# Cross-attention queries made in two steps of 128 columns in place of one step of 256

## The chip, the cores and the metric

One core of a Trainium2 chip runs the whole program. The metric is the time of one execution on the device, in microseconds; the time before is the median of three runs. The profile is of one further execution, with every instruction of the engines recorded: TensorE (PE, with its weight loads as PEld), VectorE (DVE), ScalarE (ACT), GpSimd (POOL) and SyncE (SP), which issues the transfers.

## What is computed

Two layers of a transformer block with self attention, attention to a context, and a gated feed-forward. Everything is float32. `x` is 4 x 512 x 320, the context 4 x 1601 x 192; there are 20 heads of 16.

```python
def _attn(x, ctx, wq, wk, wv, wo, bo, heads):
    q = (x @ wq).reshape(b, n, heads, dh).transpose(0, 2, 1, 3)
    k = (ctx @ wk).reshape(b, j, heads, dh).transpose(0, 2, 1, 3)
    v = (ctx @ wv).reshape(b, j, heads, dh).transpose(0, 2, 1, 3)
    sim = jnp.einsum('bhid,bhjd->bhij', q, k) * scale
    a = jax.nn.softmax(sim, axis=-1)
    out = jnp.einsum('bhij,bhjd->bhid', a, v)
    return out.transpose(0, 2, 1, 3).reshape(b, n, heads * dh) @ wo + bo
...
h1 = _ln(x, n1_g, n1_b)
x = _attn(h1, h1, q1, k1, v1, o1_w, o1_b, heads) + x
h2 = _ln(x, n2_g, n2_b)
x = _attn(h2, context, q2, k2, v2, o2_w, o2_b, heads) + x
h3 = _ln(x, n3_g, n3_b)
a, g = jnp.split(h3 @ ff_w1 + ff_b1, 2, axis=-1)
x = a * gelu(g) @ ff_w2 + ff_b2 + x
```

## The kernel before

**Units.** Attention is cut into units: one batch and one group of four heads. Each layer has 20 self units (4 batches x 5 groups), then 20 cross units, then 4 feed-forward units. A self unit has 512 keys in 4 chunks of 128, a cross unit 1601 keys in 13 chunks, the last of 65.

**Scores twice.** Each unit's scores are made twice. First as `sps` tiles (128 queries x up to 512 keys), of which DVE takes the maximum (`pm`, `nmax`); then as `st` tiles (128 keys x 512 queries), with a third product that subtracts the maximum (`nrows` by `ones`), of which ACT makes the exponential `pr`. The `sps` tiles of the next unit are made beside the `st` tiles of this one. A number is split into a high and a low part, so each tile is two products on 32 rows (and the third for `st`).

**Rounds.** `main` goes chunk by chunk. In one round it issues the `st` tiles of the chunk for four heads (12 products), mixed with four `sps` tiles of the next unit (8 products, `round_of`); then `flush` issues the product `av` of the chunk before with the values; then `steps(None, ...)` issues small steps, so that these stand between an `av` and the next round. ACT copies `av` to `vo`, and POOL adds it to `o`. For the rows of the order below, an `av` row opens a round's end: what is listed between it and the next `st` are the steps.

**Steps.** All preparation for coming units is cut into steps that wait in chains: `norm` and `scale` (layer norms), `context`, `proj` and `early` (keys, `kps`, and queries, `qps`, of cross units; both together, `qkps`, for self units), `values` (`vps`), `divide` and `project` (`ops`). A step of a chain has a cost in us, a due round, and a test whether it may run. `pace` works out from costs and due rounds how much credit a round gets; `pick` takes the head of the chain that is due first; `steps` runs it if the credit covers a share of its cost (0.5, 0.75, then 1.5 times the cost, `share`). So a smaller step needs less credit to run, and the order of all steps follows from the costs. A step's products go to one of eight PSUM banks; `bank` takes the one that a small time model (`written`, `busy`) expects to be free first. ACT copies it out.

**Queries of a cross unit.** `queries` multiplies the normed tokens `first.hT` by `wq2` for the unit's 64 columns. The 512 tokens are two halves `i` of 256, which go to two pairs of 32-row slots, so a step is 3 (rows of the contraction) x 2 x 2 = 12 products of 256 columns. In the trace each is two records, 24. ACT copies the bank with a factor to the low part of a staging tile `halves`, POOL makes of it the high and the low part (`split`, lines 827 and 828), and two transfers on SP's queue move them to `q` (`move_queries`, line 876). The moves wait for the buffer's last reader (`unread`) and `u.when` is set when all are issued; a unit's `sps` tiles start four rounds later (`at_hand`). Where the tiles are due and the queries are not made, `at_once` runs the chain and the moves on the spot.

Of the kernel before, what the change touches and what calls it, by code (L numbers as in the profile page):

```python
# [19 lines left out]
H, DH = 20, 16  # L20
# [3 lines left out]
P = 128  # L24
# [3 lines left out]
SLOT = 32  # L28
GT = GD // SLOT
# [49 lines left out]
def kernel(ctx: ExitStack, tc: tile.TileContext, x, context, ws, out):  # L79
# [18 lines left out]
    nc = tc.nc  # L98
# [314 lines left out]
    def bank(name):  # L413
        i = min(range(NB), key=lambda i: bank_free[i])
        assert bank_free[i] < HELD, name
        t = psum.tile([P, 512], F32, tag=f"bank{i}", name=name)
        bank_of[id(t)] = [i, t, bank_free[i], 0.0]
        bank_free[i] = HELD
        return t

    def written(us, *tiles):
        expect["pe"] = max([expect["pe"]] + [bank_of[id(t)][2] + 0.05 for t in tiles]) + us
        for t in tiles:
            bank_of[id(t)][3] = expect["pe"] + 0.17

    def busy(engine, us, *tiles):
        expect[engine] = max([expect[engine]] + [bank_of[id(t)][3] + 0.05 for t in tiles]) + us
        for t in tiles:
            bank_free[bank_of[id(t)][0]] = expect[engine] + 0.09
# [12 lines left out]
    def add(chain, cost, f, due, ready=yes, soon=yes):  # L442
        chains[chain].append((cost if isinstance(cost, tuple) else (cost,), due, ready, soon, f))
# [348 lines left out]
    def lead(u):  # L792

        if u.i == 0:
            return 0
        return units[u.i - (AHEAD - 1 if u.early else 2 if u.m == 0 else 1)].start
# [28 lines left out]
    def split(low, high):  # L825

        nc.gpsimd.tensor_copy(high.bitcast(F32R), low)
        nc.gpsimd.tensor_tensor(low, low, high, ALU.subtract)

    def add_proj(u):  # L830
        chain = "early" if u.early else "proj"

        due = lead(u) - (9 if u.cross else 24)
        keys_due = due - 10 if u.cross else due
        first = units[u.i - u.g]
# [26 lines left out]
        def staged(w):  # L862
            users.append(u)
            return two.tile([P, 2 * N], F32, tag="halves", name="halves")[:, : 2 * w].rearrange("p (d n) -> p d n", d=2)
# [22 lines left out]
        def staging_free():  # L887
            return len(users) < 2 or not users[-2].moves["q"] and (start["on"] or clock["round"] >= users[-2].moving["q"] + 4)

        def keys_free():  # L890
            return not pending["k"]

        def move_queries(halves, cols, may, gap):
            n = halves.shape[0]
            src = halves.rearrange("p (o d) n -> p o (d n)", o=1).to_broadcast([n, 2, 2 * halves.shape[2]])
            move("q", lambda: [(u.q.rearrange("p d n -> p (d n)")[:, cols], src)], may, gap)
# [38 lines left out]
            first.made["q"] += 1  # L935
            first.made["k"] += 1

        def queries():

            w = N // 2  # L940
            ps = bank("qps")
            written(1.41, ps)
            busy("act", 0.33, ps)
            for k, _, n in HK:
                for i in range(2):
                    for f in range(GT):
                        nc.tensor.matmul(  # L947
                            ps[(i * GT + f) * SLOT : (i * GT + f + 1) * SLOT, :w],
                            lhsT=wq2[:n, k, u.g * GD + f * SLOT : u.g * GD + (f + 1) * SLOT],
                            rhs=first.hT[:n, k, i * w : (i + 1) * w],  # L950
                            start=(k == 0),
                            stop=(k == 2),
                        )
            halves = staged(w)
            high, low = (halves[:, d] for d in range(2))
            nc.scalar.mul(low, ps[:, :w], DH**-0.5)
            split(low, high)
            for i in range(2):
                rows = slice(i * GD, (i + 1) * GD)
                move_queries(halves[rows], slice(i * N, (i + 1) * N), unread, 0 if i else GAP)  # L960
            u.keyed = True
            first.made["q"] += 1

        def keys_of_context(part):

            at, w = KCUT[part]
            ps = bank("kps")
            written(0.1 + w * 4 * 2 / 2400, ps)
            for k in range(2):
                for i in range(2):  # L970
                    for f in range(GT):
                        nc.tensor.matmul(  # L972
                            ps[(i * GT + f) * SLOT : (i * GT + f + 1) * SLOT, :w],
                            lhsT=wk2[:, k, u.g * GD + f * SLOT : u.g * GD + (f + 1) * SLOT],
                            rhs=first.kvT[:, k, i * HALF + at : i * HALF + at + w],
                            start=(k == 0),
                            stop=(k == 1),
                        )
            high, low = (room["halves"][:, d] for d in range(2))
            taken(low[:, at : at + w], ps[:, :w], ps, 0.12 + w * 0.001)  # L980
            if part + 1 < len(KCUT):
                return
            split(low, high)

            def half(i):
                return [(u.kT[:, i * HALF : (i + 1) * HALF], room["halves"][i * GD : (i + 1) * GD])]

            move("k", lambda: half(0), free, GAP + 1)
            move("k", lambda: half(1), free)
            first.made["kv"] += 1  # L990
# [7 lines left out]
        if not u.cross:  # L998
            for part in range(2):
                add(chain, (0.46,) * 3, lambda part=part: both(part), due - 2 + 2 * part, lambda part=part: part or staging_free())  # L1000
        else:
            for part, (_, w) in enumerate(KCUT):
                add(
                    chain, 0.05 + w * 8 / 2400, lambda part=part: keys_of_context(part),
                    keys_due - 2 * (len(KCUT) - 1 - part), lambda part=part: part or keys_free(),
                )
            if u.g == 0:
                add(chain, 0.0, hold, due - (6 if u.g == 0 and not u.early else 4), yes, lambda: "h" in u.own)
            add(chain, (0.477,) * 3, queries, due - (4 if u.g == 0 and not u.early else 2), staging_free)

    def taken(to, part, ps, us):

# [676 lines left out]

    add_norms(0)  # L1690
    add_proj(units[0])
    warm(5)
    until(lambda: not chains["proj"], "proj")
    at_once(units[0])
    add_proj(units[1])
    add_values(units[0])
    run("proj")
    run("proj")
    for _ in range(2 * NQ + 2):
        run("norm")  # L1700
    at_once(units[1])
    add_proj(units[2])
    first = units[0]
    first.pairs = max_pairs(first)
# [68 lines left out]
```

## Time and profile before

| | |
|---|---|
| median of three runs | 2921.99 us (2918.47 to 2926.42) |
| the profiled execution | 2916.39 us, span 2914.6 us |
| mean granted TensorE clock | 0.995 of full speed |
| cross units, first layer | about 381 to 1177 us of the span, 39 to 48 us each but for the last two |
| cross units, second layer | about 1828 to 2615 us |

Times of the trace are counted from the first instruction. A row of the timeline has start, length, engine, line, operation and tiles; records of the same kind that follow each other are put together with their count. A row of the stretches has its start and end, its length, then each engine's busy time with the number of its instructions. In a row of the groups, after the bar, stand busy time, mean length in ns, and idle time before with what ended it. In the list of waits stand the total in us, how often, and the longest.

### The profile page before, as it was taken

How to read it: one execution, taken by the hardware profiler on the slowest of the kernel's cores; microseconds unless marked ns; L12 is line 12 of the kernel's file. 1: busy time of each engine (PE TensorE's matmuls, PEld its weight loads, DVE VectorE, ACT ScalarE, POOL GpSimd, SP SyncE). 2: the span in 40 equal slices, each digit the busy share in tenths (PEclk: the TensorE clock that was granted, in tenths of full speed). 3: DMA queues.
4: the chain of work that ended last, by engine and by line, in shares of the span. 5: the costliest groups of instructions: out<-in, count | busy, mean ns of one | idle time of the engine just before them, and what ended most of it. 6: DMA issues, size and time to landing. Idle time of an engine off the chain costs nothing.

```text
span 2914.6 us, 83287 instructions
## 1 busy us (share of the span) xinstructions
PE 2860.1 (98%) x35018; PEld 1545.0 (53%) x35018; DVE 1975.7 (68%) x3752; ACT 1950.2 (67%) x4033; POOL 1299.4 (45%) x1409
## 2 busy tenths in 40 slices
PE   8999999999999999999999999999999999999999
PEld 4445555555555555355554555555555555544554
DVE  7777888788788878323257678787778878862221
ACT  3777678888888888500138776788888888893000
POOL 3656345555645545211125653455455464551100
PEclk8999999999999999999999999999999999999999
DMA  4444223232132222200113432222221122122000
GB/s 106 114 121 102 72 71 97 58 89 60 48 96 59 55 54 63 85 17 11 36 45 88 109 99 67 61 64 57 54 66 47 50 73 60 45 65 67 23 21 13
DMA packets 163495, 188.59 MB, mean 65 GB/s; under 512 B 61989, under 2 KB 109105, under 8 KB 163121
## 3 DMA queue, kind: packets, MB, share of 16 engines
q1 hardware_dynamic: 162616, 181.69, 24.4%
q8 instruction: 275, 4.51, 0.6%
q10 hardware_dynamic: 472, 1.58, 0.2%
q14 instruction: 100, 0.81, 0.1%
q0 software_dynamic: 32, 0.00, 0.0%
HBM read 55.76 MB, written 29.36 MB: 29 GB/s over the span
## 4 chain that ended last, share of the span: by engine, by line
PE 88%; DVE 4%; POOL 4%; DMA 2%; issue 1%; ACT 1%; SPq 0%; POOLq 0%; ACTq 0%; DVEq 0%
PE av L1350 22%; PE st L1324 20%; PE fps L1435 10%; PE sps L1076 9%; PE yps L1542 6%; PE vps L1035 5%; PE kps L972 4%; PE ops L1250 3%; PE qkps L908 3%; PE fps L1495 3%; DVE nmax L1087 2%; PE qps L947 2%; PE sps L1101 1%; POOL o L1370 1%; DVE pm L1087 1%
## 5 line engine op out<-in xcount | busy, mean ns | idle before, releaser
L1334 ACT ACTIVATE pr<-st 128x512 f32<-128x512 f32 (+1 forms) x2720 | 1405.0, 603 | 321.4 <-PE st L1324 292.0
L1087 DVE TENSOR_REDUCE pm<-sps 128x1 f32<-128x512 f32 (+1 forms) x1920 | 1148.3, 660 | 244.6 <-PE sps L1076 239.0
L1370 POOL TENSOR_TENSOR o<-o,vo 128x512 f32<-128x512 f32 x576 | 739.9, 1285 | 930.3 <-ACT vo L1369 909.7
L1076 PE MATMUL sps<-kT,q 32*128 32x450 f32 (+1 forms) x4800 | 870.6, 422 | 8.1 <-DMA q<-halves 4.4
L1324 PE MATMUL st<-q,kT 32*128 32x512 f32 (+1 forms) x5120 | 788.9, 419 | 0.8 <-ACT o L1364 0.4
L1350 PE MATMUL av<-pr,vals 128*32 128x512 f32 (+1 forms) x5440 | 734.2, 606 | 27.3 <-ACT pr L1334 5.4
L1324 PEld LDWEIGHTS st<-q,kT 32*128 32x128 f32 (+1 forms) x5120 | 447.0, 180 | 293.0 <-issue 112.7
L1324 PE MATMUL st<-nrows,ones 32*128 32x512 f32 (+1 forms) x2720 | 560.6, 398 | 4.5 <-DMA nrows<-turned 4.4
L1087 DVE TENSOR_REDUCE nmax<-sps 128x1 f32<-128x512 f32 x640 | 397.2, 682 | 118.0 <-PE sps L1076 114.2
L1076 PEld LDWEIGHTS sps<-kT,q 32*128 32x128 f32 x4800 | 434.0, 184 | 67.1 <-ACT pr L1334 11.7
L1369 ACT COPY vo<-av 128x512 f32<-128x512 f32 x576 | 351.7, 611 | 14.7 <-PE av L1350 8.7
L1506 ACT ACTIVATE gl<-fps,b 128x512 f32<-128x512 f32 x80 | 54.8, 687 | 408.8 <-PE fps L1495 299.1
L1435 PE MATMUL fps<-hT,w 128*128 128x512 f32 x640 | 283.1, 597 | 0.0
L1350 PEld LDWEIGHTS av<-pr,vals 128*32 128x32 f32 (+1 forms) x5440 | 111.0, 108 | 300.3 <-DVE pm L1087 185.2
L1324 PEld LDWEIGHTS st<-nrows,ones 32*128 32x128 f32 (+1 forms) x2720 | 262.3, 180 | 14.5 <-DMA nrows<-turned 6.1
L1507 DVE SCALAR_TENSOR_TENSOR hid<-fps,b,gl 128x512 f32<-128x512 f32 x80 | 59.7, 748 | 248.1 <-ACT gl L1506 246.0
L1435 PEld LDWEIGHTS fps<-hT,w 128*128 128x128 f32 x640 | 119.2, 190 | 155.1 <-issue 152.2
L1542 PE MATMUL yps<-w,hid 128*128 128x320 f32 x640 | 175.7, 434 | 0.0
L1542 PEld LDWEIGHTS yps<-w,hid 128*128 128x128 f32 x640 | 120.5, 190 | 56.3 <-ACT gl L1506 5.3
L1250 PEld LDWEIGHTS ops<-wo,aT 112*32 112x32 f32 (+1 forms) x3072 | 98.2, 110 | 59.2 <-issue 28.5
L1250 PE MATMUL ops<-wo,aT 112*32 112x160 f32 (+1 forms) x3072 | 123.8, 299 | 3.7 <-POOL aT L1232 2.7
L1111 DVE TENSOR_REDUCE pm<-sps 128x4 f32<-128x508 f32 x160 | 98.9, 680 | 37.5 <-PE sps L1101 34.8
(89 smaller groups left out, 2453.7 us busy)
## 6 DMA issues: line engine op xcount, KB each, us to landing
kT<-stages SPq DMA_DIRECT2D x80, 400.5 KB
oway<-o SPq DMA_DIRECT2D x80, 256.0 KB
q<-halves SPq DMA_DIRECT2D x80, 256.0 KB
q<-halves SPq DMA_DIRECT2D x27, 512.0 KB
kT<-halves SPq DMA_DIRECT2D x40, 256.0 KB
aT<-oway SPq DMA_DIRECT2D x32, 224.0 KB
rT<-rway SPq DMA_DIRECT2D x32, 224.0 KB
hT<-hturned SPq DMA_DIRECT2D x96, 64.0 KB
```

Of the source, the lines that this page charges most:

```text
L972: nc.tensor.matmul(ps[(i * GT + f) * SLOT : (i * GT + f + 1) * SLOT, :w], lhsT=wk2[:, k, u.g * GD + f * SLOT : u.g * GD + (f + 1) * SLOT], ...
L1035: nc.tensor.matmul(ps[f : f + m, :w], lhsT=u.kvT[:n, k, at + f : at + f + m], rhs=wv[:n, k, h0 * DH : h1 * DH], start=(k == 0), stop=(k == ...
L1076: nc.tensor.matmul(own[0][:, :w], lhsT=u.queries(slice(j * SLOT, (j + 1) * SLOT), e, t), rhs=u.kT[j * SLOT : (j + 1) * SLOT, u.k0 + at : u ...
L1087: nc.vector.tensor_reduce(to, own[0][:, :w], AX.X, ALU.max)
L1250: nc.tensor.matmul(ps[f : f + m, : D // 2], lhsT=aT[:n, k, f * NQ + t * SLOT : f * NQ + t * SLOT + m], rhs=wo[:n, k, cols], start=(k == 0) ...
L1324: nc.tensor.matmul(own[0][:r, :], lhsT=ones[rows, :r] if e == 2 else u.keys(rows, c), rhs=u.rows[rows, :] if e == 2 else u.queries(rows, e ...
L1334: nc.scalar.activation(p[:r], own[0][:r], AF.Exp)
L1350: nc.tensor.matmul(ps[j * SLOT : (j + 1) * SLOT, :], lhsT=columns_of[:r, head : head + SLOT], rhs=pr.pop((c, j))[:r, :], start=True, stop= ...
L1369: nc.scalar.copy(vo, ps)
L1370: nc.gpsimd.tensor_tensor(u.o, u.o, vo, ALU.add)
L1435: nc.tensor.matmul(ps, lhsT=w1[:, k, i * FF + c * P : i * FF + (c + 1) * P], rhs=natural(u.hT[:, k]), start=start, stop=stop,)
L1542: nc.tensor.matmul(ps[:, :D], lhsT=hid[c][:, t * P : (t + 1) * P], rhs=w2[:, c, :], start=(c == 0), stop=(c == NHC - 1),)
```

## The change

The step of 256 columns becomes two steps of 128, `queries(0)` and `queries(1)`. Each takes a bank of its own, makes 12 products of 128 columns (columns 0 to 127 of each half of 256, then 128 to 255), and has its own ACT copy into its columns of the same staging tile. Only the second runs the split and queues the moves, and only it marks the unit as keyed. The staging tile is taken by the first, which alone waits for it to be free. In the chain one entry of 3 x 0.477 = 1.431 us becomes two of 0.715 with the same due round.

```diff
-        def queries():
+        def queries(part):
 
             w = N // 2
+            cols = slice(part * P, (part + 1) * P)
             ps = bank("qps")
-            written(1.41, ps)
-            busy("act", 0.33, ps)
+            written(0.72, ps)
+            busy("act", 0.27, ps)
             for k, _, n in HK:
                 for i in range(2):
                     for f in range(GT):
                         nc.tensor.matmul(
-                            ps[(i * GT + f) * SLOT : (i * GT + f + 1) * SLOT, :w],
+                            ps[(i * GT + f) * SLOT : (i * GT + f + 1) * SLOT, :P],
                             lhsT=wq2[:n, k, u.g * GD + f * SLOT : u.g * GD + (f + 1) * SLOT],
-                            rhs=first.hT[:n, k, i * w : (i + 1) * w],
+                            rhs=first.hT[:n, k, i * w + part * P : i * w + (part + 1) * P],
                             start=(k == 0),
                             stop=(k == 2),
                         )
-            halves = staged(w)
+            if part == 0:
+                u.stage = staged(w)
+            halves = u.stage
             high, low = (halves[:, d] for d in range(2))
-            nc.scalar.mul(low, ps[:, :w], DH**-0.5)
+            nc.scalar.mul(low[:, cols], ps[:, :P], DH**-0.5)
+            if part == 0:
+                return
             split(low, high)
...
-            add(chain, (0.477,) * 3, queries, due - (4 if u.g == 0 and not u.early else 2), staging_free)
+            for part in range(2):
+                add(
+                    chain, 0.715, lambda part=part: queries(part),
+                    due - (4 if u.g == 0 and not u.early else 2), yes if part else staging_free,
+                )
```

Because the costs set the order, other steps move too. TensorE in the first layer's eleventh cross unit, its third round, before: the step stands between `av` and the round's first `st` and `sps` tiles (a row names the output and what it is made from, the output's shape, and how many follow each other).

```order
L1350 MATMUL av<-pr,vals 32x512 x4
L947 MATMUL qps<-hT,wq_113 32x256 x12
L1324 MATMUL st<-q_103,kT_101 128x512 x2
L1076 MATMUL sps<-kT_135,q_104 128x450
L1076 MATMUL sps<-kT_135,q_104 128x512
```

Of the change, TensorE in the same unit one round earlier, where no step stood before:

```order
L1359 MATMUL av<-pr,vals 32x512 x4
L948 MATMUL qps<-hT,wq_113 32x128 x12
L1333 MATMUL st<-q_103,kT_101 128x512 x2
L1085 MATMUL sps<-kT_135,q_104 128x450
L1085 MATMUL sps<-kT_135,q_104 128x512
```

The first half stands one round earlier than the wide step stood; the second half stands in that step's old round.

ACT shows several rounds in few rows, since each round has four exponentials and the copy of `av` (to `o` for a unit's first chunk, to `vo` after that), and each TensorE step has its copy behind that of `av`. The same unit's first rounds on ACT, before:

```order
L1364 COPY o<-av 128x512
L1017 COPY vals<-vps 128x8x16
L1334 ACTIVATE pr<-st 128x512 x4
L1369 COPY vo<-av 128x512
L1334 ACTIVATE pr<-st 128x512 x4
L1369 COPY vo<-av 128x512
L956 ACTIVATE halves<-qps 128x256
L1334 ACTIVATE pr<-st 128x512 x4
L1369 COPY vo<-av 128x512
L1334 ACTIVATE pr<-st 128x512 x4
```

and of the change:

```order
L1373 COPY o<-av 128x512
L1026 COPY vals<-vps 128x8x16
L1343 ACTIVATE pr<-st 128x512 x4
L1378 COPY vo<-av 128x512
L959 ACTIVATE halves<-qps 128x128
L1343 ACTIVATE pr<-st 128x512 x4
L1378 COPY vo<-av 128x512
L959 ACTIVATE halves<-qps 128x128
L1343 ACTIVATE pr<-st 128x512 x4
L1378 COPY vo<-av 128x512
```

Of the four rounds, two held no step before; now one does. The second place is ACT one unit earlier, the tenth cross unit, from the end of the ninth. Before:

```order
L1334 ACTIVATE pr<-st 128x512 x4
L1364 COPY o<-av 128x512
L956 ACTIVATE halves<-qps 128x256
L1334 ACTIVATE pr<-st 128x512 x4
L1369 COPY vo<-av 128x512
L1334 ACTIVATE pr<-st 128x512 x4
L1369 COPY vo<-av 128x512
L1334 ACTIVATE pr<-st 128x512 x4
L1369 COPY vo<-av 128x512
L1017 COPY stages<-kps 128x201
```

and of the change:

```order
L959 ACTIVATE halves<-qps 128x128
L1343 ACTIVATE pr<-st 128x512 x4
L1373 COPY o<-av 128x512
L1343 ACTIVATE pr<-st 128x512 x4
L1378 COPY vo<-av 128x512
L959 ACTIVATE halves<-qps 128x128
L1343 ACTIVATE pr<-st 128x512 x4
L1378 COPY vo<-av 128x512
L1343 ACTIVATE pr<-st 128x512 x4
L1378 COPY vo<-av 128x512
L1026 COPY stages<-kps 128x201
```

The first half went ahead to the last round of the unit before, and the second half one round later than the wide step; the round of the copy to `o` and the one before `stages` hold no step.

## The prediction

> **What bounds the kernel now.** I read the page first: the busy shares, then the chain that ended last.
>
> ```profile
> span 2914.6 us, 83287 instructions
> PE 2860.1 (98%) x35018; PEld 1545.0 (53%) x35018; DVE 1975.7 (68%) x3752; ACT 1950.2 (67%) x4033; POOL 1299.4 (45%) x1409
> PE 88%; DVE 4%; POOL 4%; DMA 2%; issue 1%; ACT 1%; SPq 0%; POOLq 0%; ACTq 0%; DVEq 0%
> ```
>
> TensorE is busy for 98% of the span and holds 88% of the chain, so a gain must come out of TensorE's own time. ACT and DVE show about two thirds over the whole span, but that is a mean over stages. So the second view is the busy time by stretches. I cut the cross units into rounds, from the first `av` matmul of one chunk to the first of the next, and kept the 443 rounds that hold 12 `st` and 8 `sps` tiles. A round's steps stand right behind its `av`. I put the rounds in classes by those steps and took the stretches of a class together; the last row of that view, the sum, is shown for each: 70 rounds without a step that follow a round with one; 30 without a step that follow another without; 101 with one `kps` step alone; 47 with one `vps` step of 192 columns alone; 29 with the `qps` step alone.
>
> ```profile
> sum 195.61, PE 195.44 PEld 95.29 DVE 190.95 ACT 193.63 POOL 90.71; mean PE 2.79 PEld 1.36 DVE 2.73 ACT 2.77 POOL 1.30
> sum 79.54, PE 79.23 PEld 37.49 DVE 69.58 ACT 74.94 POOL 43.76; mean PE 2.64 PEld 1.25 DVE 2.32 ACT 2.50 POOL 1.46
> sum 318.19, PE 313.98 PEld 166.64 DVE 254.01 ACT 273.60 POOL 169.80; mean PE 3.11 PEld 1.65 DVE 2.51 ACT 2.71 POOL 1.68
> sum 149.37, PE 145.42 PEld 78.39 DVE 126.44 ACT 126.65 POOL 90.47; mean PE 3.09 PEld 1.67 DVE 2.69 ACT 2.69 POOL 1.92
> sum 108.99, PE 108.11 PEld 55.58 DVE 70.24 ACT 81.73 POOL 66.36; mean PE 3.73 PEld 1.92 DVE 2.42 ACT 2.82 POOL 2.29
> ```
>
> A round of the first class takes 195.61/70 = 2.79 us, and ACT is busy for 2.77 us of it and DVE for 2.73: such an empty round goes at the pace of ACT and DVE, and TensorE's modelled busy time hides the waits. An empty round behind another takes 79.54/30 = 2.65. A `kps` round takes 318.19/101 = 3.15 with ACT at 2.71, a `vps` round 149.37/47 = 3.18, a `qps` round 108.99/29 = 3.76 with ACT at 2.82: there TensorE sets the pace. The waits that say the same stand in the list of waits:
>
> ```profile
> PEld av L1350 <- DVE pm L1087: 185.2, 419, 2.4
> PEld st L1324 <- ACT pr L1334: 114.6, 146, 0.8
> ```
>
> So a step costs TensorE its own length, but in an otherwise empty round part of it fills time in which TensorE would wait.
>
> **The change part by part.** First, what a step of 128 columns costs TensorE. The program has its twin: the self units' `vps` step has the same 12 products with 128, 96 and 96 rows and 128 moving columns. From the timeline, TensorE: an `av` and the next `st` around the `qps` step of 256 columns, around that `vps` step, and with nothing between.
>
> ```profile
> 265.26 1.06 PE L1350 MATMUL av<-pr,vals 128*32 128x512 f32 x8
> 266.14 1.48 PE L947 MATMUL qps<-hT,wq 128*32 128x256 f32 x24
> 267.56 0.50 PE L1324 MATMUL st<-q,kT 32*128 32x512 f32 x2
> ...
> 80.68 1.06 PE L1350 MATMUL av<-pr,vals 128*32 128x512 f32 x8
> 81.56 0.84 PE L1035 MATMUL vps<-wv,hT 128*32 128x128 f32 x24
> 82.33 0.49 PE L1324 MATMUL st<-q,kT 32*128 32x512 f32 x2
> ...
> 2222.15 1.06 PE L1350 MATMUL av<-pr,vals 128*32 128x512 f32 x8
> 2223.15 0.50 PE L1324 MATMUL st<-q,kT 32*128 32x512 f32 x2
> ```
>
> From `av` to `st` it is 2.30 us with the wide step, 1.65 with the narrow, 1.00 with none. So 256 columns cost 1.30 us, 128 columns 0.65, and two narrow steps 1.30 again. The rows' hundredths leave at most 0.02 us per unit for 12 more matmul calls (24 more records); I take 0.01, which over 40 units is +0.4 us, with 0 and +0.8 as ends. [...]
>
> A round has one further fixed price, the turn from `av` and steps (128 rows by 32 columns) to `st` (32 by 128): `av` to `qps` takes 0.88 us, `av` to `st` 1.00, so 0.12. It is paid once in every round, with a step or without, so a second step in another round adds none. [...]
>
> Second, ACT. A copy of 256 columns becomes two of 128. The nearest row for 128 columns is that of the values' copy.
>
> ```profile
> L956 ACT ACTIVATE halves<-qps 128x256 f32<-128x256 f32 x40 | 15.4, 385 | 19.4 <-PE qps L947 19.4
> L1017 ACT COPY vals<-vps 128x128 f32<-128x128 f32 x128 | 36.7, 297 | 15.6 <-PE vps L1035 12.0 <-DVE nmax L1087 2.8
> ```
>
> 2 x 297 - 385 = 209 ns a unit, 8.4 us over 40. Hidden where it falls: a round with a `kps` step has the same kind of copy behind it and ACT still idles 3.15 - 2.71 = 0.44 us. I take 0; with that cover gone the end is +8.4. DVE gets nothing. POOL's split of high and low and the two `q` moves on SP stay whole and stand behind the second half, so there are as many of them. They move, by nought to five rounds, in both directions; on SP they pass transfers of keys, weights and `nrows`.
>
> Third, the order, which is where the sum comes from. 29 of the 40 units get their halves in two rounds, 11 in one. Counting rounds of the kind above in the two orders: empty ones go from 100 to 76, those behind a step from 70 to 58, those behind another empty one from 30 to 18. (Not 29 fewer: some halves stand beside a `vps` or `ops` step, and other steps shift too.) What is a round worth that gets a step? With the step's own length taken off, a `kps` round (0.68: `av` at 2219.00, `st` at 2220.68) is 3.15 - 0.68 = 2.47, a `vps` round of 192 columns, whose 8 products of 96 rows also last 0.65, 3.18 - 0.65 = 2.53.
>
> ```profile
> 2219.00 1.06 PE L1350 MATMUL av<-pr,vals 128*32 128x512 f32 x8
> 2220.68 0.50 PE L1324 MATMUL st<-q,kT 32*128 32x512 f32 x2
> ```
>
> I take 2.50, between them. Then 12 x (2.79 - 2.50) = 3.5 us and 12 x (2.65 - 2.50) = 1.8 us are saved: -5.3. The places shown with the change differ in this: in the first the two halves fill two rounds of which one was empty; in the second the first half goes one unit ahead, and of the two empty rounds behind the wide step one stands. The sum: -5.3 + 0.4 + 0 = -4.9 us, or -0.17%. The self units' rounds hold the same steps in both orders but for two, where neighbouring `kps` widths change place, and the feed-forward ones the same: 0.
>
> The profiled execution took 2916.39 us (span 2914.6 and 1.8 around it), so it would take 2911.5. It lies 5.6 us below the median of the runs, 2921.99; the forecast is for the median: 2921.99 - 4.9 = 2917. A change of less than about 0.3%, 8.8 us, is not told from none by runs that spread from 2918.47 to 2926.42.
>
> **The rivals.** (1) Nothing is gained, because ACT and DVE set the pace over several rounds and a filled round only moves the wait. For it: an empty round behind another, 2.65, already costs less than one behind a step, 2.79, so part of the wait is a debt that the step before left. Against it: a unit's long run of `kps` and `vps` rounds shows no such debt, ACT 2.7 of 3.15. Time: 2922 + 0.4 = 2922.
>
> (2) More is gained. All 29 split units, and what shifts with them, fill rounds at the full price: 40 x (2.79 - 2.47) = 12.8 us, 2909. Against it: the order's own count of 24.
>
> (3) Slower, by late queries. A unit's scores for its maxima start four rounds after its `q` is moved; if they start too late, the rest is made up in a burst in one chunk. Before, this happens in three chunks; the timeline's stretches show one (third row: the normal case with its `kps` step; the first is a round without `sps`):
>
> ```profile
> 543.95:545.85 1.90, 1.90 (x21) 0.65 (x21) 1.86 (x4) 1.87 (x4) 1.82 (x3) 1.00 0.00 0
> 581.79:586.62 4.83, 4.78 (x78) 2.95 (x77) 3.37 (x7) 4.04 (x9) 3.54 (x4) 1.00 0.01 3
> 586.62:590.11 3.49, 3.39 (x30) 1.62 (x28) 3.39 (x9) 1.91 (x5) 2.35 (x2) 1.00 0.00 0
> 2230.86:2234.43 3.57, 3.54 (x70) 2.39 (x69) 2.10 (x5) 2.78 (x7) 1.93 (x2) 1.00 0.00 0
> 2234.43:2237.57 3.14, 3.11 (x45) 1.66 (x45) 2.40 (x5) 2.60 (x6) 1.20 (x1) 1.00 0.00 0
> ```
>
> The burst and the round behind it take 4.83 - 0.68 + 3.49 = 7.64 without the `kps` step; the normal two 3.57 + 3.14 - 2 x 0.68 = 5.35; and the burst's extra tiles had left one round at 1.90 in place of some 2.47. So a late unit costs 7.64 - 5.35 - 0.57 = 1.7 us. Eight more late units would cost 13.6 us and with the gain end at 2931. Against it: the order has three bursts still, and although five units of the 40 start their maxima one chunk later, only `q`'s landing in time could make more of them. The second half could also hold a bank longer than the planner's 0.72 and 0.27 us say, in 69 rounds at 0.1 us; that ends near 2924, inside the band.
>
> **How the numbers follow.** The forecast of some 5 us less: 0.52. Nothing gained (1): 0.22. More gained (2): 0.16. Slower (3): 0.10. Faster by over 0.3% takes (2) and the tail of the forecast, 0.05: 0.21. Slower by over 0.3% takes (3) and nearly nothing of (1): 0.11. Within 0.3%: 0.68. The range goes from 2908, below rival (2), to 2929: rival (1) with the copies' +8.4 end would be 2930, and a late unit or two beside the gain are inside.
>
> **What would show it.** Right: `qps` records of 128 columns, 1920 in all, with `av` to `st` around one half at 1.65 us; ACT's `qps` copies at 80 times 250 to 300 ns; the empty cross rounds 76 in number at 2.7 to 2.8 us each; rounds with a half step alone at 3.12 to 3.2 us; the list of waits with less on "PEld st from ACT pr". Wrong: half-step rounds above 3.3 us (the wait moved, rival 1); empty rounds that got longer; more than three chunks of 4.1 us and over without their steps (rival 3); or a whole stage outside the cross units that moved, which I count at nothing.

## The result and the profile after

| | before | changed |
|---|---|---|
| median, first set of runs | 2921.11 us (2918.47 to 2926.42, 6 runs) | 2912.07 us (2909.44 to 2915.55, 6 runs) |
| ratio, 95% interval | | 0.9966 [0.9956, 0.9976] |
| profiled execution, span | 2916.39, 2914.6 us | 2914.06, 2912.3 us |

The change makes the kernel about 9 us faster, 0.34%. The forecast of 2917 us had the sign and about half the size. Of all executions reported below one is left out as disturbed: 3409 us at a mean clock of 0.752, of the kernel with one step in each cross round. The page of the changed kernel, then its list of waits, then the groups of the queries' matmuls and copies:

```profile
span 2912.3 us, 85212 instructions
PE 2857.3 (98%) x35978; PEld 1569.9 (54%) x35978; DVE 1977.9 (68%) x3752; ACT 1954.8 (67%) x4073; POOL 1301.7 (45%) x1409
PE 87%; DVE 5%; POOL 3%; DMA 2%; issue 1%; ACT 1%; SPq 0%; POOLq 0%; ACTq 0%; DVEq 0%
```

```profile
PEld av L1359 <- DVE pm L1096: 191.3, 428, 1.7
PEld st L1333 <- ACT pr L1343: 99.4, 128, 0.8
```

```profile
L948 PE MATMUL qps<-hT,wq 96*32 96x128 f32 x1280 | 49.8, 272 | 0.0
L948 PE MATMUL qps<-hT,wq 128*32 128x128 f32 x640 | 32.2, 272 | 0.0
L959 ACT ACTIVATE halves<-qps 128x128 f32<-128x128 f32 x80 | 24.6, 307 | 5.9 <-PE qps L948 5.3
```

There are 1280 + 640 = 1920 records of 128 columns and 80 copies. ACT's copies cost 24.6 - 15.4 = 9.2 us more than the 40 wide ones. TensorE's wait for the exponentials fell from 114.6 to 99.4 us. A half step in its round, on the timeline of TensorE:

```profile
813.36 1.07 PE L1359 MATMUL av<-pr,vals 128*32 128x512 f32 x8
814.25 0.84 PE L948 MATMUL qps<-hT,wq 128*32 128x128 f32 x24
815.02 0.50 PE L1333 MATMUL st<-q,kT 32*128 32x512 f32 x2
```

From `av` to `st` it is 1.66 us. The rounds of the cross units, classed as before, each class's sum from the view by stretches: 58 without a step behind a round with one; 18 without a step behind another such; 105 with one `kps` step alone; 45 with one half step of the queries alone.

```profile
sum 161.49, PE 161.43 PEld 78.17 DVE 158.13 ACT 161.44 POOL 77.42; mean PE 2.78 PEld 1.35 DVE 2.73 ACT 2.78 POOL 1.33
sum 49.09, PE 48.88 PEld 23.50 DVE 45.06 ACT 44.51 POOL 23.54; mean PE 2.72 PEld 1.31 DVE 2.50 ACT 2.47 POOL 1.31
sum 330.42, PE 326.17 PEld 173.00 DVE 260.98 ACT 283.46 POOL 184.52; mean PE 3.11 PEld 1.65 DVE 2.49 ACT 2.70 POOL 1.76
sum 140.29, PE 139.13 PEld 82.84 DVE 107.84 ACT 120.03 POOL 65.57; mean PE 3.09 PEld 1.84 DVE 2.40 ACT 2.67 POOL 1.46
```

That is 2.78, 2.73, 3.15 and 3.12 us a round: no empty round got much longer, and a half step of 0.65 makes a round of 3.12, so that the round beside it costs 2.47. All the rounds of the cross units together, as two stretches with their sum, of before and then of the changed kernel:

```profile
sum 1639.12, PE 1621.63 PEld 886.37 DVE 1291.23 ACT 1395.11 POOL 862.11; mean PE 810.81 PEld 443.19 DVE 645.61 ACT 697.56 POOL 431.05
```

```profile
sum 1633.99, PE 1616.47 PEld 907.46 DVE 1293.14 ACT 1399.50 POOL 863.48; mean PE 808.23 PEld 453.73 DVE 646.57 ACT 699.75 POOL 431.74
```

The cross units became 1639.12 - 1633.99 = 5.1 us shorter, where the forecast said 4.9. So the sum foreseen is there, and some 4 us more came from elsewhere. But the sum hides that the two layers differ. Their rows, before and then changed:

```profile
381.18:1204.84 823.66, 812.00 (x11489) 443.74 (x11489) 653.70 (x1207) 697.88 (x1469) 431.04 (x409) 1.00 0.28 70
1827.69:2643.15 815.46, 809.63 (x11465) 442.63 (x11465) 637.53 (x1164) 697.24 (x1469) 431.06 (x409) 1.00 0.24 60
386.62:1205.67 819.05, 808.71 (x11921) 453.95 (x11921) 654.01 (x1207) 699.64 (x1487) 431.77 (x409) 1.00 0.28 71
1825.87:2640.81 814.94, 807.76 (x11913) 453.50 (x11913) 639.14 (x1164) 699.86 (x1488) 431.71 (x409) 1.00 0.24 60
```

The first layer gained 4.6 us and the second 0.5, though 13 of the 24 empty rounds went in the first and 11 in the second, which by the forecast's 5.3 us for the 24 would be some 2.9 and 2.4. Other rounds changed too. In the first layer, for one, a wait of TensorE for DVE is 1.29 us in place of 2.02, in a round that holds one key step more; in the second, a round with an `ops` step takes 4.43 us in place of 3.28, of which 0.75 is a new wait for DVE. That the sum comes this close to the forecast is in part luck.

### Where the rest came from: the second self layer and the granted clock

Each run lists TensorE's mean granted clock. Before: 0.9937 over 27 runs. Changed: 0.9951 over 11 (6 and 5, means 0.9948 and 0.9954). If a lower clock cost its full share of the time everywhere, a span times its mean clock would be the time at full clock: 2901.6 us before, 2895.7 changed (standard errors 0.5 and 0.7). By that reckoning, of the 10.0 us between the means (2921.8 and 2911.8), 5.9 would be work and waits, and 0.0014 x 2915 = 4.1 the clock.

The reckoning gives the clock too much, since the mean also holds the start, where a low clock cost little. Ahead of its first `av` TensorE is at half clock for 23.9 us in the first trace of the change and for 13.7 in its second, and that `av` starts at 52.3 and 50.9 us: 10.2 us fewer at half clock save 1.4 us, not 5.1. And a line fitted through the 88 runs of before on record falls by 1.4 us for each 0.001 of clock, not by 2.9. By that slope, an estimate, 0.0014 is some 2 us.

The traces show what a lower mean is made of: single stretches of some 3.4 us, or two together, at a granted clock of 0.50. Some stand behind a wait of TensorE, not all: near 1504 us, in the first traces of both kernels, the clock fell though no wait of TensorE in the 13 us ahead is above 0.4 us (before, it is busy for 13.25 of the 13.6 us ahead). From the view by stretches (the number after POOL's is the granted clock), before, in the 18th self unit of the second layer, where the first row holds a wait of 0.76 us for `nrows`:

```profile
1784.00:1787.20 3.20, 2.03 (x24) 0.78 (x20) 2.87 (x6) 1.50 (x4) 3.17 (x3) 1.00 0.10 36
1787.20:1790.60 3.40, 3.40 (x36) 1.62 (x32) 1.02 (x2) 1.66 (x4) 1.12 (x1) 0.50 0.20 63
1790.60:1793.00 2.40, 2.40 (x48) 1.48 (x40) 0.53 (x1) 0.97 (x3) 0.14 (x1) 0.99 0.00 0
```

and the same place of the changed kernel:

```profile
1782.65:1787.74 5.09, 4.58 (x53) 2.09 (x52) 5.09 (x9) 3.53 (x9) 3.06 (x4) 1.00 0.24 68
1787.74:1792.30 4.56, 4.48 (x77) 2.63 (x76) 2.16 (x5) 3.08 (x8) 2.09 (x2) 1.00 0.13 47
```

The round that holds this stretch (`av` at 1786.97, the next at 1793.22) takes 6.25 us, and 4.57 with the same steps in the changed kernel, so these 3.4 us at a granted clock of 0.50 cost 1.7 us. For the other such stretches where TensorE sets the pace, 1.7 us each is an estimate from this pair. In the record of the clock in these two traces, every low stretch behind the first 57 us is at 0.50 and 3.41 us long, or 6.83, but for the last, which the end of the span cuts off.

One trace is a sample. After its first 57 us, the profiled execution of before has two such stretches and that of the change five, so these two spans lie only 2.3 us apart where the medians lie 9. Of the second traces, taken with the runs repeated below, before has four and the change none.

### The profile page after: what moved, and what is told of

The parts are those of the page before. It is cut to its first block, busy times and chain, and to the rows that moved or that the text cites. A ratio compares the mean times of both kernels' runs of the same rounds, so it can differ in the third digit from the quotient of the medians.

```text
span 2912.3 us, 85212 instructions
## 1 busy us (share of the span) xinstructions
PE 2857.3 (98%) x35978; PEld 1569.9 (54%) x35978; DVE 1977.9 (68%) x3752; ACT 1954.8 (67%) x4073; POOL 1301.7 (45%) x1409
## 3 DMA queue, kind: packets, MB, share of 16 engines
q1 hardware_dynamic: 162616, 181.69, 24.6%
## 4 chain that ended last, share of the span: by engine, by line
PE 87%; DVE 5%; POOL 3%; DMA 2%; issue 1%; ACT 1%; SPq 0%; POOLq 0%; ACTq 0%; DVEq 0%
PE av L1359 22%; PE st L1333 20%; PE fps L1444 10%; PE sps L1085 9%; PE yps L1551 6%; PE vps L1044 5%; PE kps L977 4%; PE ops L1259 4%; PE qkps L908 3%; PE fps L1504 3%; DVE nmax L1096 2%; PE qps L948 2%; DVE pm L1096 1%; PE sps L1110 1%; POOL o L1379 1%
## 5 line engine op out<-in xcount | busy, mean ns | idle before, releaser
L1085 PE MATMUL sps<-kT,q 32*128 32x512 f32 (+1 forms) x4800 | 862.7, 421 | 9.0 <-DMA q<-halves 4.4
```

What stands on the lines that cost most here:

```text
L1085: nc.tensor.matmul(own[0][:, :w], lhsT=u.queries(slice(j * SLOT, (j + 1) * SLOT), e, t), rhs=u.kT[j * SLOT : (j + 1) * SLOT, u.k0 + at : u ...
```

## The experiments

Two theories stood after the result. A: in the cross units a narrow step fills a round that ACT and DVE set, and the gain is the price of those rounds; the rest is something else. B: a second source outside the cross units, which belongs to the other order or timing and not to chance. Most runs take A apart; the last one tests a part of what B became, the clock.

**Both kernels again**

> The change as it is, once more, for a narrower interval and a second trace. Theory A (all of the gain is the 24 cross rounds that are no longer empty): cross rounds some 5 us shorter than before in this trace too, and a ratio of 0.998, so that part of the 9 us measured first is scatter. Theory B (a second source beside these rounds, in the self units or in the moved q transfers, gives as much again): ratio 0.9966 again, and a stage other than the cross units shorter by 3 us or more in both traces.

> The kernel before, unchanged, for a second trace of it: ratio 1.000. Theory A: its cross rounds sum to within 2 us of the first trace of it, and what differs between the two traces lies in the self units, where waits for transfers (nrows, aT) come and go by 1 to 3 us. Theory B: the self units' stage is as in the first trace within 1 us.

The change: 2909.68 us (2906.22 to 2917.15, 5 runs) beside 2922.36, ratio 0.9965 [0.9951, 0.9979]. Before: 2920.91 (11 runs), 0.9994 [0.9985, 1.0003]. The gain is no chance. The cross units took 1640.2 and 1634.7 us, about 1 us from the first traces; of the former, 1.7 are one half-clock stretch. Before's first and second self layers scatter by 3 and by nothing, but the second self layer of the change took 319.1 and 317.8 us where before took 321.9 twice. That is the second source, 3.5 us on the mean, and the rounds show its parts, within 0.1 us alike in both pairs of traces. In the 18th unit two rounds take 11.9 us before and 9.6 changed: 1.7 of this is the half-clock stretch shown above, the rest mostly the wait ahead of it. From the 19th unit's first round on, seven rounds together take 31.2 us before and 30.3 changed: one `vps` step of 16 records has left them for the cross units (656 such records in the second self layer, 672 before; 1552 in the cross units behind it, 1536 before), and `ops` steps stand in other rounds.

**The narrow step without the new order, and the new order without the narrow step**

The first runs both halves at the wide step's place; the second plans with two entries, and does the whole wide step in the second. Both are shown against the changed kernel.

```diff
-            for part in range(2):
-                add(chain, 0.715, lambda part=part: queries(part), ...)
+            add(chain, (0.477,) * 3, lambda: (queries(0), queries(1)), ...)
```

```diff
         def queries(part):
+            if part == 0:
+                return
...
-            written(0.72, ps)
+            written(1.41, ps)
```

> The two half steps with a bank and a copy each, but run one behind the other in the one place of the wide step; one chain entry of 3 x 0.477 us as before, so every other step stands where it stood and 100 cross rounds stay empty. Theory A: nothing gained, +0 to +0.8 us on TensorE, ratio 1.000 (0.999 to 1.001). Rival C (the gain is the narrower step itself: a bank is let go sooner, and ACT's copy starts after half the products): ratio 0.997 to 0.998 as for the change.

> The chain entries, costs and due rounds of the change, so that the other steps and the q moves shift as in the change, but the first entry does nothing and the second makes the wide step of 256 columns whole. 97 cross rounds are empty (65 behind a step, 32 behind another empty one) against 100 before and 76 in the change. Theory A: -5 x 0.29 + 2 x 0.15 = -1.2 us, ratio 0.9996. Theory B and any other in which the other steps' new places or the q moves give the gain: ratio 0.997 to 0.998.

The halves at one place: 2918.7 us (11 runs), 0.9991 [0.9982, 1.0000]; the order alone: 2916.0 (11 runs), 0.9981 [0.9972, 0.9990]. The sum of the cross units' stretches, for the halves at one place and then for the order alone:

```profile
sum 1640.69, PE 1623.72 PEld 907.41 DVE 1291.86 ACT 1398.10 POOL 862.24; mean PE 811.86 PEld 453.70 DVE 645.93 ACT 699.05 POOL 431.12
```

```profile
sum 1638.06, PE 1621.02 PEld 889.47 DVE 1293.64 ACT 1396.63 POOL 862.02; mean PE 810.51 PEld 444.73 DVE 646.82 ACT 698.32 POOL 431.01
```

Two narrow steps at one place cost what one wide step does: 1640.7 us holds one half-clock stretch, and without its 1.7 it is 1639.0, before's figure. The span times the clock is 2901.2 us, as before. The second copy and the second bank are hidden, and rival C's 0.997 to 0.998 lies outside the interval. The order alone brings 1.1 us in the cross units, forecast 1.2. Neither part gives the change's 5 there: it takes halves and separate rounds.

Over the whole execution, though, the order alone gained 0.19%, 5.5 us, where theory A had 0.9996, which lies outside the interval; theory B's 0.998 lies in it. Its trace shows the second source in part: the same `vps` step has left the second self layer, and near 1787 us there is no half-clock stretch. Its mean clock was 0.9950.

**What a filled round costs**

Both kernels are the change with one more step of 12 products of 128 columns, on constant data, whose output nothing reads. The first puts it in cross rounds that hold no step, the second in 86 rounds that hold one step of about half length already (60 key steps, 26 half steps of the queries).

```diff
             steps(None, 1 if extra or c == u.nch - 1 else 2)
+            if u.cross and not last and not extra and tiles == 4 and not ran:
+                filler()
```

```diff
-            if ... and not ran:
+            if ... and len(filled) < 86 and len(ran) == 1 and 0.705 < ran[0] < 0.73:
```

> The change plus 86 needless steps: 12 products of 128 columns of a constant into a bank that nobody reads, behind the av wherever a cross round with four sps tiles ran no step. 74 of them fall into the 76 empty rounds of the kind counted, the other 12 ahead of rounds with other tiles. The steps' order is that of the change. Theory A (an empty round waits some 0.27 us for ACT and DVE, which a step fills): 74 x (0.65 - 0.27) + 12 x 0.65 = +36 us over the change, some 2948 us, ratio to the kernel before 1.009. Rival E (the wait is owed by the rounds before and comes back later): 86 x 0.65 = +56 us, 2968 us, ratio 1.016.

> The same 86 needless steps in 86 rounds of the change that ran one kps step or one half step of the queries; the 76 empty rounds stay. Theory A and rival E alike: TensorE sets the pace there, so each costs its whole 0.65 us, +56 us, some 2968 us, ratio 1.016. The difference to the other placing is the price of the waits: 20 us by theory A, 0 by rival E.

In empty rounds: 2945.16 us (5 runs), 1.0080 [1.0068, 1.0092]. In rounds with a step: 2964.29 (4 runs), 1.0147 [1.0133, 1.0162]. The sum over the 74 filled rounds of the first kernel of the class's kind:

```profile
sum 230.48, PE 228.39 PEld 135.77 DVE 184.76 ACT 187.48 POOL 118.82; mean PE 3.09 PEld 1.83 DVE 2.50 ACT 2.53 POOL 1.61
```

and over the second kernel's 86 filled rounds and its 76 empty ones:

```profile
sum 325.33, PE 323.17 PEld 204.73 DVE 215.52 ACT 230.38 POOL 167.26; mean PE 3.76 PEld 2.38 DVE 2.51 ACT 2.68 POOL 1.94
sum 210.66, PE 210.39 PEld 101.97 DVE 203.35 ACT 205.90 POOL 92.57; mean PE 2.77 PEld 1.34 DVE 2.68 ACT 2.71 POOL 1.22
```

The same 0.65 us takes a round from 2.77 to 230.48/74 = 3.11, that is 0.34 more, but from 3.14 (60 rounds of 3.15 and 26 of 3.12) to 325.33/86 = 3.78, that is 0.64 more. Taken against the same rounds of the change it is 0.36 and 0.64. So some 0.3 us a step is hidden in a round that ACT and DVE set and nothing elsewhere; the two kernels lie 19.1 us apart, forecast 20. The wait that a step filled did not come back in a later round.

**Which steps fill a round: keys in six parts, queries in four**

```diff
-KCUT = slices(HALF, 4)
+KCUT = slices(HALF, 6)
```

```diff
-            cols = slice(part * P, (part + 1) * P)
+            m = P // 2
+            cols = slice(part * m, (part + 1) * m)
...
-            for part in range(2):
+            for part in range(4):
                 add(
-                    chain, 0.715, lambda part=part: queries(part),
+                    chain, 0.358, lambda part=part: queries(part),
```

> The change carried on to the keys: the context's keys of a unit in six steps of 133 or 134 columns in place of four of 200. Empty cross rounds go from 76 to 46 (28 behind a step, 18 behind another). Theory A with its prices by the length of the step (a round with a step of 0.4 to 0.5 us costs 2.53 beside it, with 0.65 or more 2.47): 30 empty rounds fewer give -8 us, some 110 more rounds with a short step in place of a long one take 6 of it back: -2 us on the change, ratio to before 0.996. If a short step fills a round as well as a long one: -8 us, ratio 0.994. Rival E: no difference to the change, 0.9966.

> The queries in four steps of 64 columns, a bank and a copy each, entries of 0.358 us. Empty cross rounds go on down, from 76 to 63 (43 behind a step, 20 behind another), but 42 rounds now hold a step under 0.4 us alone, against 7, and five units are made up in a burst, against three. Theory A with its prices by the step's length (2.69 us beside a step under 0.4 us, 2.47 beside 0.65 and more, 2.79 and 2.70 for the empty ones): the cross rounds' sum is 6 us above the change's, some 2918 us, ratio to before 0.9986. Rival (what counts is that a round is not empty, however short the step): 13 fewer empty rounds, -4 us on the change, ratio 0.995.

Keys in six: 2930.48 us (8 runs), 1.0031 [1.0019, 1.0043]; a gain had been forecast. Quarters: 2931.37 (5 runs), 1.0032 [1.0020, 1.0045], some 20 us above the change where theory A had 6: its sign against the change, but three times its size, and its ratio to before, 0.9986, was missed. Part of both losses is a wait that neither forecast held. The list of waits has, for keys in six and for quarters:

```profile
PE sps L1085 <- ACT stages L1026: 8.4, 4, 3.5
```

```profile
PE sps L1086 <- ACT stages L1027: 3.6, 2, 2.4
```

What ACT waited for stands on its timeline, with keys in six:

```profile
2028.08 0.62 ACT L1378 COPY vo<-av 128x512 f32<-128x512 f32 x1
2031.74 0.27 ACT L1026 COPY stages<-kps 128x134 f32<-128x134 f32 x1 [3.04 <-DMA kT<-stages]
2031.91 1.59 ACT L1343 ACTIVATE pr<-st 128x512 f32<-128x512 f32 x3
```

The copy of the keys stands ahead of the exponentials on ACT and waits 3.04 us for the transfer of earlier keys out of its staging tile; in the same microseconds two moves of `q`, 256 KB each, are issued on SP's queue. TensorE waits with it, and the clock then falls (first row the wait, second what follows, same kernel):

```profile
2028.60:2032.00 3.40, 0.65 (x11) 0.33 (x3) 1.22 (x2) 0.36 (x3) 1.26 (x1) 0.97 0.76 216
2032.00:2035.40 3.40, 3.34 (x25) 1.32 (x29) 1.29 (x2) 2.12 (x6) 0.00 (x0) 0.50 0.01 3
```

DMA is busy for 0.76 of the first stretch, at 216 GB/s. The rest is the price of the short steps: 117 rounds with one short key step of 0.46 us, and 37 with one quarter step of 0.335:

```profile
sum 360.18, PE 350.67 PEld 202.79 DVE 289.37 ACT 311.15 POOL 169.88; mean PE 3.00 PEld 1.73 DVE 2.47 ACT 2.66 POOL 1.45
```

```profile
sum 110.17, PE 108.67 PEld 65.16 DVE 91.52 ACT 98.96 POOL 50.24; mean PE 2.94 PEld 1.76 DVE 2.47 ACT 2.67 POOL 1.36
```

Beside the step these rounds cost 2.62 and 2.64 us on the mean, not 2.50, but the mean hides two kinds. With keys in six, three rounds hold the wait above, and without them it is 2.53, as priced. Of the 37 rounds with a quarter step, six took 3.1 to 3.9 us (one with a wait of 0.60 us for `nrows`; in three ACT's copy of `av` waits 0.97, 0.51 and 0.48 us until POOL has added the one before); the other 31 took 89.02/31 = 2.87, 2.54 beside the step. So a short step does fill a round: 2.77 becomes 2.87 for 0.335 us of work. What was missed in both is not the length of the step but what its company waits for.

Keys in six: by span times clock 2904.2 us, 8.5 more than the change, near the 8.4 us of waits for the copies of keys; the rest goes with its clock, 0.9915, though by that reckoning the clock's part is an upper bound. Quarters: the cross units took 1652.4 us, 18 more than the change's, where 6 had been forecast. Named in the trace are three half-clock stretches (3 x 1.7 = 5.1 us), the keys' copies (3.6), the six long rounds (6 x (3.5 - 2.87) = 3.8) and five bursts in place of three (2 x 1.7); these come to 16. That any step will do, however short, is refuted by the time; that a short step fills its round badly is not what the rounds show either.

**Other shares of credit**

Three kernels are the change with other numbers in `share`: the first step of a round free of credit; one step a round where possible, in all units; and the same in cross units alone.

```diff
-... else (0.5, 0.75, 1.5)
+... else (-1.0, 0.75, 1.5)
```

```diff
-... else (0.5, 0.75, 1.5)
+... else (0.2, 2.0, 3.0)
```

```diff
-... else (0.5, 0.75, 1.5)
+... else (0.2, 2.0, 3.0) if clock["cross"] else (0.5, 0.75, 1.5)
```

> The change, and a round's first step runs whatever the credit is (share of -1.0 in place of 0.5; credit is never under -2): steps go one round earlier. Empty cross rounds 70 (46 behind a step, 24 behind another), three bursts as in the change, step lengths as in the change. Theory A: -2 us on the change by its prices, ratio to before 0.996. Rival E: no difference, 0.9966.

> The change with shares 0.2, 2.0 and 3.0 in place of 0.5, 0.75 and 1.5, so that a second step in a round needs four times its credit: empty cross rounds 64 (42 behind a step, 22 behind another), four bursts. Theory A: -3 us on the change by its prices, ratio to before 0.9955; if it holds, this is the faster version of the two kernels. Rival E: no difference, 0.9966.

> As the run with shares 0.2, 2.0 and 3.0, but in cross units alone; self units keep 0.5, 0.75 and 1.5, so their rounds hold the same steps as in the change. Empty cross rounds 65 (44 behind a step, 21 behind another), three bursts as in the change. Theory A: 11 fewer empty rounds, -3 us on the change by its prices, cross rounds' sum some 1631 us, ratio to before 0.9955, and the 10 us that the self units lost in the earlier run are not lost here. Rival F (moving steps one round earlier makes keys' copies wait for their staging tile again, as in the runs with six key steps and four query steps, and that eats the gain): cross rounds' sum 1635 us or more.

They gave 2911.2 us (6 runs), 0.9969 [0.9957, 0.9980]; 2918.36 (11 runs), 0.9990 [0.9981, 0.9999]; and 2918.71 (11 runs), 0.9985 [0.9977, 0.9994]. The first kernel's cross units, as a sum:

```profile
sum 1632.48, PE 1611.55 PEld 902.75 DVE 1291.83 ACT 1395.54 POOL 862.24; mean PE 805.78 PEld 451.38 DVE 645.91 ACT 697.77 POOL 431.12
```

They are 1.5 us shorter than the change's, forecast 2, which the whole execution cannot show. The second and third forecasts failed. The shares also apply in the self units, where the second kernel's first layer took 337.7 us against 329 to 334. In the third the self units keep their shares, and its span times its clock, 0.9934, is 2896.5 us, the change's figure. Its cross units took 1640.4 us in the trace, where theory A had 1631 and rival F 1635 or more. F's number came, but not F's cause: no wait of TensorE for a copy of keys is on its list. The trace shows where they lost: `av` waits 2.51, 1.94 and 1.93 us for DVE's `pm` in the first layer's third, eighth and thirteenth cross units, where the change has 0.75, 1.29 and 1.29. List of waits of the change, then of this kernel, then the stretch behind the first of the three:

```profile
PE av L1359 <- DVE pm L1096: 5.2, 8, 1.3
```

```profile
PE av L1359 <- DVE pm L1096: 9.5, 11, 2.5
```

```profile
481.30:484.90 3.60, 1.09 (x21) 0.66 (x14) 3.53 (x7) 2.17 (x5) 3.27 (x5) 0.95 0.48 113
484.90:488.50 3.60, 3.60 (x32) 1.43 (x36) 1.73 (x3) 0.90 (x2) 1.41 (x4) 0.57 0.85 192
```

Three such half-clock stretches stand in its cross units, some 5.1 us, and these three waits are 3.1 us longer than the change's, which more than covers the 6.4 us by which its cross units are longer. No version beats the change by more than the runs can tell.

**The clock alone**

Before, with nine steps of 0.65 us on constant data put at five places where TensorE waits: three in self units, and the eighth and thirteenth cross units of the first layer. It adds work and takes none away.

```diff
+    AFTER = {(0, "self", 14, 1): 1, (0, "self", 17, 3): 2, (1, "self", 17, 3): 1}
+    AHEAD_OF = {(0, "cross", 7, 1): 3, (0, "cross", 12, 1): 2}
...
+            for _ in range(AHEAD_OF.get((u.l, u.kind, u.m, c), 0)):
+                filler()
             flush()
...
             steps(None, 1 if extra or c == u.nch - 1 else 2)
+            for _ in range(AFTER.get((u.l, u.kind, u.m, c), 0)):
+                filler()
```

> The kernel before plus nine needless steps of 0.65 us at five places where TensorE waits 0.8 to 2.0 us in its traces (self units 14 and 17 of the first layer, 17 of the second, cross units 7 and 12 of the first layer), for transfers, for o or for DVE. Theory D (the change gains some 4 us beside the rounds because fewer of these waits let the TensorE clock fall to 0.5 for a stretch of 3.4 us): granted clock of the runs from 0.9937 to some 0.995, no stretch of half clock at 344, 689 and 1788 us, ratio 0.9985. Rival (the stretches come whatever TensorE does there): same clock, and the steps cost 0 to 6 us, ratio 1.000 to 1.002.

2918.74 us (11 runs), 0.9990 [0.9981, 0.9998]: 2 to 3 us faster, just clear of noise, by a kernel that only does more (nine steps are 5.9 us). Its mean clock was 0.9953, that of before in the same set of runs 0.9938. Only four of the nine steps lie in a wait, those in the self units: two of the three rounds there became 0.7 us shorter in spite of them (5.69 to 4.99 at the place shown above, 6.32 to 5.64 near 340 us), the third stayed as it was. The five in the cross units stand behind the wait, for they wait for DVE themselves, and their two rounds became 3.6 and 1.3 us longer:

```profile
PE dps L519 <- DVE pm L1104: 3.3, 2, 2.0
```

The place shown above, in its trace:

```profile
1784.00:1787.20 3.20, 3.20 (x36) 1.51 (x36) 3.19 (x7) 2.60 (x7) 1.29 (x1) 1.00 0.32 113
1787.20:1790.60 3.40, 3.26 (x65) 2.12 (x68) 3.40 (x6) 1.40 (x4) 3.02 (x3) 1.00 0.22 69
```

TensorE is busy there and the half-clock stretch is gone. The one near 688 us, where the steps did not fill the wait, stands. Near 344 us, in the first layer's 18th self unit, all 14 traces together say more. In 13 of them TensorE waits there for 1.2 to 1.8 us for `nrows`; in ten one or two half-clock stretches follow, in three none (the first trace of before and the second of the change among these). In the one left, this kernel's, the wait is 0.48 us and no stretch follows. So behind such waits the stretches came often, but not each time. How much of this kernel's gain is the clock and how much its shorter rounds was not separated.

## Why the prediction was right or wrong

**The half step's price: right.** 0.66 us by the timeline, against 0.65, and 1.66 from `av` to `st`. The kernel with both halves at one place shows that 24 more records add nothing that a stage of 1639 us tells.

**ACT's copies: right that they are hidden**, though 307 ns in place of 250 to 300 and 9.2 us more in all; with the +8.4 end the cross units of that same kernel would have been at 1647, and they are at 1639.0 without the half-clock stretch.

**The empty rounds: right.** 76, at 2.78 and 2.73; a half-step round at 3.12. The saving of 5.3 became 5.1 to 5.5 by the pairs of traces (3.7 with the half-clock stretch of before's second taken off). But it lies nearly all in the first layer (4.6 and 5.4 us, against 0.5 and 0.1 in the second): the price holds for a round of its class, and what other rounds gain and lose beside it, which the forecast put at nothing, happened to cancel.

**Rival 1, a wait that only moves: refuted** by the two filled kernels: 0.34 us against 0.64 for the same work, with the empty rounds left at 2.77.

**Rival 2, 2909 by 29 units at full price: not what happened**, though the time came near it. The count of empty rounds was 24 fewer, and the cross units gave 5; the rest of the 9 came from the second self layer.

**Rival 3, bursts: not in the change**, whose bursts are three as before. With quarters they became five; beside them, the kernels with more and shorter steps showed ACT waiting for a staging tile's transfer (3.04 us in the one shown).

**The step that failed** is the one that set everything outside the cross units at 0 ("The self units' rounds hold the same steps in both orders but for two ...: 0"). The second self layer became 2.8 and 4.1 us shorter in the two pairs of traces. The order was misread: a `vps` step left the second layer's 19th unit for the cross units, one moved by two rounds in the first layer, and `ops` steps shifted, which together made seven rounds of the second layer 0.9 us shorter. Nor are the waits the same: in the 18th unit one of 0.76 us for `nrows` is gone, and with it the stretch at half clock behind it, 2.3 us in all. The sum was made in time at full clock, with no term for a wait or for the clock. The view by stretches of before has the rows for such a term: two stretches at 0.50. The forecast notes that the profiled execution lay 5.6 us below the median and does not ask why; before's second trace, nearer the median, has two more such stretches.

What stays open. The mean clock of the change is 0.0014 higher (standard error 0.0006, and each run lists it to 0.001 only). The one stretch near 1790 us, in both traces of before and in neither of the change, is 1.7/2915 = 0.0006 of it; the rest has no place in these traces, and may be the start or chance. That stretch is missing too with both halves at one place, so a shift in timing is enough and the new order is not needed; why that `nrows` wait is gone was not settled. Why the other rounds of the cross units gained in the first layer and lost in the second was followed in two rounds only. Nor is a stretch at half clock certain behind a wait: before waits 2.0 us for DVE near 687 us in both traces, and only the second has the fall:

```profile
685.20:688.50 3.30, 1.29 (x24) 0.84 (x26) 3.23 (x5) 2.54 (x6) 3.06 (x5) 1.00 0.02 5
688.80:692.20 3.40, 3.40 (x32) 1.71 (x28) 1.40 (x3) 0.90 (x2) 1.83 (x9) 0.50 0.45 85
```

Why the fall came in one execution and not in the other was not shown.

## What to carry to other kernels

Price a small step by the round that it lands in: where ACT and DVE set a round, 0.65 us of TensorE's work cost 0.34, and beside another step 0.64, and a wait that was filled did not come back. Before splitting finer, ask for what the steps' copies wait (here a staging tile whose transfer had not ended), since here a copy that stood ahead of the exponentials and waited 3.04 us stopped TensorE. Count the steps of every stage in both orders, since a step that moves from one stage to another changes both. And look at the granted clock in small stretches and in more than one trace: here a wait of 0.76 us was followed by a stretch at half clock that cost 1.7 us more, and a difference between two spans can be that alone.

## What the hardware showed that I had not expected

Waits of 0.8 to 2.5 us, in a program whose TensorE is busy for 98% of the span, were followed by 3.4 us or twice that at a granted clock of 0.50, one such wait in ten traces of 13. A kernel with 5.9 us more work ran 0.1% faster, at a mean clock of 0.9953 in place of 0.9938. At the start of the program 10.2 us fewer at half clock saved only 1.4 us. And 24 more matmul records a unit for the same columns, 960 in all, cost nothing that these runs can show: with both halves at one place the cross units took 1639.0 us without their half-clock stretch, and 1639.1 before.
